# Rolled overflow path, fewer parts before and behind a branch, attention queries two batches at a time

## The chip, the cores and the metric

The kernel runs on one core of a Trainium2 chip. The core has five engines that work side by side: TensorE (PE, matrix products; its weight loads are the row PEld), VectorE (DVE), ScalarE (ACT), GpSimd (POOL) and SyncE (SP, which here only starts transfers). Transfers are carried by 16 DMA engines. The metric is device time in microseconds, lower is better; one execution was also taken by the hardware profiler.

## The reference

The reference is a transformer of two layers on x (8 batches of 100 rows, 512 wide), with a context of 8 x 361 rows, 128 wide. Each of its four parts is added to x after a layer normalisation:

- attention 1: 16 heads of 32, causal, keys and values from the first 100 rows of the context;
- a mixture of 8 experts: a gate takes the two best of 8 scores of each row, and y = sum of w_e * (silu(x W1_e) * (x W2_e)) W3_e, hidden width 352;
- attention 2: 16 heads; its queries go through Wq, w_kc_q and W_qr, its keys are the rotated context through W_kr, softmax over 361 rows, values through w_kc_kv and Wo;
- a feed-forward part with a gate, hidden width 1408, weights and rows quantised to 8-bit steps.

## The kernel before

**Tiling.** The 800 rows are seven tiles, six of 128 and one of 32 (`ROWS`). Products are in float32, so that each product is two passes on PE in the profile. Results land in eight PSUM banks (`bank`), from which ACT or DVE copies them; `evacuate` gives them to the two in turn.

**Order.** Up to the branch, and again from behind it to the end of attention 2's projections, the order on PE, DVE and ACT is that of the source (`manual_schedule`). The order on SP and POOL, and that of attention 2's loop, is made by the scheduler of the framework. Each queue runs in order.

**Attention 1.** Two products on zeros stand ahead of everything. `queries0(b, n, parts)` makes the queries of n batches, in one or two banks; batches 0 and 1 are made one by one with 100 columns, the others in pairs with 200.

**Gate and slots.** `rank_choices` finds each row's two experts on DVE, `give_slots` counts a place for each choice in the 240 slots of its expert (`CAP`), and POOL writes the rows to these slots in DRAM (`x_slot`) with indirect transfers, one for each tile and choice: ten for tiles 0 to 4, then four for tiles 5 and 6. DVE then computes `spilt`: whether an expert has more than 240 rows.

**The branch.** PE, DVE, ACT and POOL read `spilt` (`values_load`, L879) and jump (`If`, L886). The path behind the condition computes the mixture in a general way, written out for 8 experts x 7 tiles; with these inputs it isn't taken. Past the branch, SP fetches the slots of experts 0 and 1 (`fetch`, L960).

**Folding.** The weights Wq, w_kc_q and W_qr of attention 2 are multiplied into one matrix `wqf`, two heads (a pair) at a time, between other work. A pair has three parts: `fold_first` (L705, and the copy a_p), `fold_second` (L723, and the copy f_p), `fold_third` (transposes, L733). `fold_load` loads the weights of a pair, three pairs ahead at most. Pair 0 is folded ahead of the branch, pair 1's first part too; pair 1's other parts and pair 2 behind it; pairs 3 to 7 within experts 0 to 4.

**Experts.** For each expert: `gate_and_up(0)`, (1), (2) (L1053), then the transposed rows of the next expert (`columns_of`, L985), then the down product (L1117). Between them DVE quantises weights of the last part: rows of gate and up (`quantise_next`), and in experts 0 to 3 a quarter of w_down, `quantise_down(*down_in)`, which was loaded into a single buffer `dn` (L828) and is turned by a transfer (L150). `load_expert(e + 2)` comes when expert e has used its weights.

**Attention 2.** A batch has 1600 rows (16 heads x 100) in 13 tiles. For a tile: scores (L1312), maximum (L1314), exponential (L1318), division on POOL or DVE (L1321), transposes (L1327), evacuation to pT; each 400 columns of pT give a product with the context (L1333). Work behind the scores is three tiles late. The queries of the next batch are made by `queries(b + 1)` at tile 8 (in batch 0 at tile 2), with L1300: 64 rows, two heads in two halves of the array, 100 columns.

## Time and profile before

| | us |
|---|---|
| median of 3 runs | 683.59 (680.39 to 683.71) |
| the profiled execution | 684.2 |
| its span | 682.5 |
| queries of batches 0 and 1 (L269, 100 columns) | 10.25 to 17.5 |
| last PE work before the branch | 126.6 |
| PE goes on | 134.65 |
| first fetch of slots issued | 135.79 |
| expert 0 starts | 144.27 |
| expert 5 starts | 238.58 |
| attention 2's loop | about 347 to 537 |

The span is what the engines show between the first and the last instruction; the execution's time has 1.7 us more around it. A row of the profile's groups gives the line, the engine, the operation, the tile written and those read, the shapes and the count. "Idle before" is how long the engine stood still ahead of it, and what released it. The clock row gives the share of its full clock that PE was granted. A row that ends in q (PEldq, SPq) is that of an engine's sequencer, which starts instructions and runs branches.

### The profile page before, as it was taken

What the parts mean: (1) busy time and instruction counts of PE and PEld (TensorE: products, weight loads), DVE (VectorE), ACT (ScalarE), POOL (GpSimd) and SP (SyncE); (2) the same over time, 40 slices, a digit from 0 to 9 for tenths busy, and PEclk for the clock granted to TensorE, in tenths of its full rate; (3) what the DMA queues carried; (4) which work ended last, traced back from release to release, by engine and by line L of the source; (5) the groups of instructions that cost most, each with busy time, mean ns of one, the idle gap of its engine ahead of it and who ended that gap; (6) DMA issues with size and microseconds to landing.
All of it is one profiled execution on the core that took longest, in us unless ns stands there. A gap on an engine that the chain in (4) does not pass through costs nothing.

```text
span 682.5 us, 10210 instructions
## 1 busy us (share of the span) xinstructions
PE 647.0 (95%) x3637; PEld 417.3 (61%) x3637; DVE 420.7 (62%) x1059; ACT 245.2 (36%) x557; POOL 184.1 (27%) x197
## 2 busy tenths in 40 slices
PE   8999997499998999999999999999999999999995
PEld 6767755367765677568866666666666644444442
DVE  4875698326665453254168877776676356566687
ACT  3654444141221211231155555455555322221140
POOL 2222231601110022138424243324333102221021
PEclk9999999589999999999999999999999999999998
DMA  8700293699999999664200211110000120111211
GB/s 303 237 17 18 99 331 108 244 301 190 271 288 321 322 254 275 131 193 122 63 1 17 57 44 42 31 35 12 1 11 1 46 83 8 30 29 30 49 37 61
DMA packets 80312, 80.41 MB, mean 118 GB/s; under 512 B 41283, under 2 KB 54135, under 8 KB 80127
## 3 DMA queue, kind: packets, MB, share of 16 engines
q1 hardware_dynamic: 76543, 70.97, 35.8%
q0 software_dynamic: 3712, 8.72, 6.6%
q8 instruction: 30, 0.49, 0.3%
q14 instruction: 27, 0.22, 0.1%
HBM read 56.36 MB, written 16.50 MB: 107 GB/s over the span
## 4 chain that ended last, share of the span: by engine, by line
PE 65%; DVE 7%; DMA 3%; POOL 2%; issue 2%; ACT 1%; SPq 0%; POOLq 0%; ACTq 0%; DVEq 0%
PE bank L357 12%; PE bank L1053 10%; PE bank L1333 10%; PE bank L1312 7%; PE bank L1267 6%; PE bank L1117 5%; PE bank L1327 4%; PE bank L1457 3%; POOL e L1321 2%; PE bank L1300 2%; DVE nm L1314 1%; PE bank L705 1%; PE bank L723 1%; DMA dn<-in_wdn 1%; PE bank L985 1%
## 5 line engine op out<-in xcount | busy, mean ns | idle before, releaser
L1321 POOL TENSOR_SCALAR e<-e,rs 128x361 f32<-128x361 f32 (+1 forms) x56 | 67.3, 1203 | 134.9 <-DVE rs L1320 134.2
L357 PE MATMUL bank<-wvo,ctxT 128*128 128x512 f32 x192 | 83.9, 593 | 0.0
L1312 PE MATMUL bank<-kvT,qe 128*128 128x361 f32 (+1 forms) x208 | 82.0, 477 | 0.0
L1053 PE MATMUL bank<-xgT,w 128*128 128x240 f32 (+1 forms) x384 | 76.5, 371 | 1.6 <-ACT xgT L989 0.9
L1053 PEld LDWEIGHTS bank<-xgT,w 128*128 128x128 f32 (+1 forms) x384 | 63.8, 181 | 16.7 <-issue 9.0
L1333 PE MATMUL bank<-pT,kvr 121*128 121x400 f32 x192 | 70.4, 502 | 1.8 <-DVE pT L80 1.8
L1318 ACT ACTIVATE e<-bank,nm 128x361 f32<-128x361 f32 (+1 forms) x104 | 58.7, 564 | 29.8 <-DVE nm L1314 21.0
L1327 PEld LDWEIGHTS bank<-ident,e 128*121 128x121 f32 (+1 forms) x312 | 47.3, 183 | 33.7 <-POOL e L1321 7.8
L1314 DVE TENSOR_REDUCE nm<-bank 128x1 f32<-128x361 f32 (+1 forms) x104 | 54.9, 528 | 20.3 <-PE bank L1312 19.2
L357 PEld LDWEIGHTS bank<-wvo,ctxT 128*128 128x128 f32 x192 | 36.2, 190 | 43.1 <-issue 42.6
L1128 POOL DMA_INDIRECT x_acc<-y,place x16 | 24.4, 1525 | 128.5 <-ACT y L1127 125.0
L1327 PE MATMUL bank<-ident,e 128*121 128x128 f32 (+1 forms) x312 | 52.8, 279 | 2.1 <-POOL e L1321 2.1
L1474 POOL TENSOR_TENSOR hid<-g,u 128x512 f32<-128x512 f32 (+1 forms) x17 | 20.5, 1214 | 111.1 <-ACT g L1465 74.8
L1333 PEld LDWEIGHTS bank<-pT,kvr 121*128 121x128 f32 x192 | 33.9, 190 | 21.3 <-issue 1.9
L1117 PE MATMUL bank<-w,hT 128*128 128x512 f32 (+3 forms) x96 | 43.3, 596 | 2.2 <-DVE hT L1077 2.2
L1267 PE MATMUL bank<-xT,wqf 128*128 128x256 f32 (+1 forms) x192 | 43.8, 389 | 0.7 <-ACT xT L1252 0.7
L322 POOL TENSOR_TENSOR s<-s,rs 100x800 f32<-100x800 f32 x16 | 24.4, 1523 | 71.2 <-DVE rs L321 30.5
L1267 PEld LDWEIGHTS bank<-xT,wqf 128*128 128x128 f32 x192 | 36.2, 190 | 7.4 <-ACT xT L1252 0.9
L1312 PEld LDWEIGHTS bank<-kvT,qe 128*128 128x128 f32 (+1 forms) x208 | 32.5, 186 | 9.4
L82 ACT COPY pT<-bank 121x384 f32<-121x384 f32 (+1 forms) x51 | 23.7, 465 | 31.9 <-PE bank L1327 31.3
L80 DVE COPY ctxT<-bank 128x400 f32<-128x400 f32 (+2 forms) x23 | 13.2, 574 | 34.1 <-PE bank L1267 24.8
L1117 PEld LDWEIGHTS bank<-w,hT 128*128 128x128 f32 (+3 forms) x96 | 16.8, 183 | 22.9 <-issue 16.4
(251 smaller groups left out, 1020.2 us busy)
## 6 DMA issues: line engine op xcount, KB each, us to landing
w<-in_w SPq DMA_DIRECT2D x8, 1408.0 KB
gu<-in_wgu SPq DMA_DIRECT2D x22, 256.0 KB
w<-in_w SPq DMA_DIRECT2D x16, 256.0 KB
wq_p<-in_wq SPq DMA_DIRECT2D x8, 512.0 KB
wo<-in_wo SPq DMA_DIRECT2D x8, 512.0 KB
x_slot<-zeros SPq DMA_DIRECT2D x1, 3840.0 KB
kq_p<-in_wkcq SPq DMA_DIRECT2D x16, 192.0 KB
dn<-in_wdn SPq DMA_DIRECT2D x4, 704.0 KB
```

The source lines that it names most:

```text
L322: nc.gpsimd.tensor_tensor(part, part, rs.unsqueeze(2).to_broadcast([S, 8, S]), ALU.mult)
L357: nc.tensor.matmul(po[:, :D], lhs[:, c, ds(t * P, r)], rhs[:, c, :], start=(c == 0), stop=(c == chunks - 1),)
L1053: nc.tensor.matmul(po, w12_e[:, c, cols], xgT[:, c, :], start=(c == c0), stop=(c == c1 - 1))
L1117: nc.tensor.matmul(py[i][:n], hT[:mr, m, ds(s0, n)], w3_e[:mr, m, :], start=(m == 0), stop=(m == 2))
L1128: d = nc.gpsimd.indirect_dma_start(out=x_acc, out_offset=bass.IndirectOffsetOnAxis(ap=place[:, 0:1], axis=0), in_=y, in_offset=None, compu ...
L1267: nc.tensor.matmul(pq[:, i, :], wqf[:, c, ts(p0 + i, P)], xT[:, c, :], start=(c == 0), stop=(c == KC - 1),)
L1312: nc.tensor.matmul(ps[:r, :L], qe[:, ds(k0, r)], kvT, start=True, stop=True)
L1314: d = nc.vector.tensor_reduce(nm[:r], ps[:r, :L], AX.X, ALU.max, negate=True)
L1318: nc.scalar.activation(e[:r], ps[:r, :L], AF.Exp, bias=nm[:r], accum_out=sm[:r])
L1321: (nc.vector if odd else nc.gpsimd).tensor_scalar_mul(e[:r], e[:r], rs[:r])
L1327: nc.tensor.transpose(pt[:LP, c, :r], e[:r, ds(c * (LP - 1), LP)], ident[:r, :r])
L1333: nc.tensor.matmul(pc[:, :VC], kvr[:, c, :], pT[:, c, ts(j, VC)], start=(c == 0), stop=(c == LC - 1))
```

## The change

- **Attention 1**: the queries of batches 0 and 1 are made together, 200 columns each; a third product on zeros stands at the start.
- **Scatter**: for the last tile (32 rows) the second choices are copied under the first, rows and places, and one transfer of 64 rows writes both: 13 transfers, not 14.
- **Folding**: pair 1 is finished ahead of the branch; two whole pairs (2 and 3) stand behind it; four pairs (4 to 7) stay in experts 0 to 3. Those four are made by `fold_beside`: the two heads in two column halves of the array, with 128 columns moving, which gives the transposed product; `fold_turn` turns it back. Their parts stand one place later in an expert.
- **Branch**: the general path is two nested loops at run time instead of 56 written-out blocks, with gathered weights and rows; the other side of the branch is placed behind it (`preferred_fallthrough_block=True`), and SP reads `spilt` and branches too. A Silu of one column is computed by ACT between.
- **Attention 2**: `queries` makes two batches at a time (200 columns), in four parts; two parts at tiles 6 and 9 of every second batch. pT is two halves with three buffers in turn, and the tile that lies across column 800 is evacuated in two pieces.

The arithmetic for these inputs is the same apart from the order in which the folded product is formed. The order on SP comes out differently in the experts: in the built program `wq_p` of a pair and the first weights of expert e + 2 now stand ahead of the turned quarter of w_down and the next load of `dn` in experts 1 and 2, where they stood behind them.

```diff
@@ -429,7 +431,7 @@
-    for _ in range(2):
+    for _ in range(3):
...
     take_columns(1)
-    queries0(0, 1)
-    queries0(1, 1)
+    queries0(0, 2)
     first_norm(2, NT)
...
+
+        if t1 == NT:
+            r = ROWS[-1]
+            nc.vector.tensor_copy(x_all[ds(r, r), NT - 1, :], x_all[:r, NT - 1, :])
+            nc.vector.tensor_copy(to_i[0][ds(r, r), NT - 1 :], to_i[1][:r, NT - 1 :])
         for t in range(t0, t1):
-            r = ROWS[t]
-            for k in range(2):
+            r = ROWS[t] if t < NT - 1 else 2 * ROWS[t]
+            for k in range(2 if t < NT - 1 else 1):
                 d = nc.gpsimd.indirect_dma_start(
...
+    def fold_beside(i, wq_p, kq_p, qr_p):
+        pa = bank()
+        for c in range(CQ // P):
+            for j in range(2):
+                nc.tensor.matmul(
+                    pa[ds(R1 * j, R1), :P], qr_p[:, j, c, :], kq_p[:, j, c, :],
+                    start=(c == 0), stop=(c == CQ // P - 1),
+                )
+        t_p = fw.tile([P, P], F32, tag="t_p", name=f"t_p{i}", bufs=1)
+        nc.scalar.copy(t_p, pa[:, :P])
+        return i, wq_p, t_p
+
+    def fold_turn(i, wq_p, t_p):
+        pa = bank()
+        nc.tensor.transpose(pa[:, :P], t_p, ident)
+        a_p = fw.tile([P, P], F32, tag="a_p", name=f"a_p{i}", bufs=2)
+        nc.scalar.copy(a_p, pa[:, :P])
+        return i, wq_p, a_p
...
     fold_third(*part)
     gate_scores(5, 7, xT)
-    loads = loaded.pop(0)
-    pa = fold_head(*loads, 0)
+    part = fold_first(*loaded.pop(0))
     rank_choices(5, 7)
     give_slots(5, 7)
     nc.vector.tensor_reduce(most, pn[:, :NE], AX.X, ALU.max)
     spilt = gp.tile([P, 1], I32, tag="spilt", name="spilt")
     nc.vector.tensor_scalar(spilt, most, float(CAP), None, ALU.is_gt)
+    part = fold_second(*part)
+    fold_third(*part)
     close_atw()
     close_at()
...
         spilt[0:1, 0:1], min_val=0, max_val=1,
         engines=[
             mybir.EngineType.PE, mybir.EngineType.DVE, mybir.EngineType.Activation,
-            mybir.EngineType.Pool,
+            mybir.EngineType.Pool, mybir.EngineType.SP,
         ],
     )
-    with tc.If(spills > 0, preferred_fallthrough_block=False):
+    with tc.If(spills > 0, preferred_fallthrough_block=True):
+
+
         sp, close_sp = open_pool("spill", side="right")
...
+        with tc.For_i(0, NE, 1, hint_engines=()):
+            nc.gpsimd.iota(at_x, pattern=[[0, 1]], base=0, channel_multiplier=1)
+            w12_e = sp.tile([P, KC, 2 * HE], F32, tag="spw", name="spw")
+            for c in range(KC):
...
+            with tc.For_i(0, NT, 1, hint_engines=()):
+                x_t = sp.tile([P, D], F32, tag="spx", name="spx")
+                gathered(x_t, x_all_rows, at_x)
...
-    part = fold_copy(*loads, fold_head(*loads, 1, pa))
+    nc.scalar.activation(most, ln_eps, AF.Silu)
+    part = fold_first(*loaded.pop(0))
     following = fold_first(*loaded.pop(0))
     part = fold_second(*part)
     following = fold_second(*following)
...
         part = None
         gate_and_up(0)
         if loaded:
-            part = fold_first(*loaded.pop(0))
+            part = fold_beside(*loaded.pop(0))
             if pairs_left:
                 loaded.append(fold_load(pairs_left.pop(0)))
         quantise_next()
         gate_and_up(1)
         if part:
-            part = fold_second(*part)
+            part = fold_turn(*part)
         if e < KC:
             turn_down(*quantise_down(*down_in))
             if e + 1 < KC:
                 down_in = load_down(e + 1)
         gate_and_up(2)
+        if part:
+            part = fold_second(*part)
         quantise_next()
         if e + 2 < NE:
             experts[e + 2] = load_expert(e + 2)
         else:
             load_wo(*((0, 1, 2) if e + 2 == NE else (3, 4)))
-        if part:
-            fold_third(*part)
         if e == KC + 1:
             load_wo(5, 6, 7)
         if e + 1 < NE:
             turned = columns_of(e + 1, slots[e + 1])
             gates_next = choices(e + 1, slots[e + 1])
+        if part:
+            fold_third(*part)
...
-    def queries(b):
-        qe = a1w.tile([P, 2, HP * S], F32, tag="qe", name=f"qe{b}")
-        for half in range(2):
+
+    def pair_tile(b):
+        return a1w.tile([P, 2, 2, HP * S], F32, tag="qe", name=f"qe{b}")
+
+    def queries(b, qe, parts):
+        for part in parts:
             pe = [bank(), bank()]
-            for i in range(4):
+            for i in range(2):
                 for par in range(2):
                     nc.tensor.matmul(
-                        pe[par][:, ts(i, S)], wkr_sb[ds(R1 * par, R1), 4 * half + i, :],
-                        qr[ds(R1 * par, R1), 4 * half + i, ts(b, S)], start=True, stop=True,
+                        pe[par][:, ts(i, 2 * S)], wkr_sb[ds(R1 * par, R1), 2 * part + i, :],
+                        qr[ds(R1 * par, R1), 2 * part + i, ds(b * S, 2 * S)],
+                        start=True, stop=True,
                     )
-            nc.vector.tensor_copy(qe[:, 0, ts(half, VC)], pe[0][:, :VC])
-            nc.scalar.copy(qe[:, 1, ts(half, VC)], pe[1][:, :VC])
-        return qe.rearrange("p a q -> p (a q)")
+            for par, copy in ((0, nc.vector.tensor_copy), (1, nc.scalar.copy)):
+                copy(
+                    qe[:, :, par, ds(2 * part * S, 2 * S)].rearrange("p b (i q) -> p i b q", i=2),
+                    pe[par][:, : 4 * S].rearrange("p (i b q) -> p i b q", i=2, b=2),
+                )
+
+    def of_batch(qe, k):
+        return qe[:, k].rearrange("p a q -> p (a q)")
...
-        evacuate(pT[:, :, ds(k0, r)], pt[:LP, :, :r])
+        for half in range(2):
+            c0, c1 = max(k0, half * 2 * VC), min(k0 + r, (half + 1) * 2 * VC)
+            if c0 < c1:
+                evacuate(
+                    pT[half][:, :, ds(c0 - half * 2 * VC, c1 - c0)], pt[:LP, :, c0 - k0 : c1 - k0]
+                )
     def values(b, j, kvr, pT):
+        pT = pT[j // 2][:, :, ts(j % 2, VC)]
         pc = bank()
         for c in range(LC):
             nc.tensor.matmul(
-                pc[:, :VC], kvr[:, c, :], pT[:, c, ts(j, VC)], start=(c == 0), stop=(c == LC - 1)
+                pc[:, :VC], kvr[:, c, :], pT[:, c, :], start=(c == 0), stop=(c == LC - 1)
...
-    qe = queries(0)
+    pair = pair_tile(0)
+    queries(0, pair, range(HP // 2))
+    qe = of_batch(pair, 0)
     for b in range(B):
         more = b + 1 < B
-        pT = a1w.tile([LP, LC, BROWS], F32, tag="pT", name=f"pT{b}")
+        pT = [
+            a1w.tile([LP, LC, 2 * VC], F32, tag="pT", name=f"pT{b}_{half}", bufs=3)
+            for half in range(2)
+        ]
         if more:
             kvr_next = context_rows(b + 1)
         for i, (k0, r) in enumerate(BTILES):
             e = scores(qe, kvT, k0, r, i % 2)
             late.append(lambda a=(b, i, e, kvr, pT): behind(*a))
             drain(3)
-            if more and i == (8 if b else 2):
-                qe_next = queries(b + 1)
+            if more and b % 2 and i in (6, 9):
+                if i == 6:
+                    pair_next = pair_tile(b + 1)
+                queries(b + 1, pair_next, range(2) if i == 6 else range(2, HP // 2))
...
-            qe, kvr, kvT = qe_next, kvr_next, kvT_next
+            if b % 2:
+                pair = pair_next
+            qe, kvr, kvT = of_batch(pair, (b + 1) % 2), kvr_next, kvT_next
```

## The prediction

> **What bounds the kernel now.** I read the page first, then stretches of it, then single waits and the order of the built programs. The page's busy row and the clock in its 40 slices:

> ```profile
> PE 647.0 (95%) x3637; PEld 417.3 (61%) x3637; DVE 420.7 (62%) x1059; ACT 245.2 (36%) x557; POOL 184.1 (27%) x197
> PEclk9999999589999999999999999999999999999998
> ```

> TensorE carries the span, and the only hole before the tail is around slice 8: the branch. Time saved on TensorE is time of the kernel wherever TensorE waits for nobody, so I ask for each touched stretch whether it does. These rows are start:end, length, busy time of PE, PEld, DVE, ACT, POOL, the granted clock, the DMA share and GB/s:

> ```profile
> 10.14:17.30 7.16, 7.16 (x67) 7.16 (x66) 4.01 (x10) 1.09 (x2) 0.00 (x0) 1.00 1.05 351
> 126.60:134.65 8.05, 0.01 (x1) 0.00 (x1) 2.18 (x15) 0.00 (x0) 5.57 (x6) 0.50 0.56 203
> 199.05:220.31 21.26, 18.69 (x89) 12.74 (x89) 11.83 (x30) 3.72 (x8) 3.57 (x3) 1.00 1.13 300
> 220.31:238.58 18.27, 18.27 (x88) 12.98 (x89) 8.67 (x29) 3.69 (x8) 2.50 (x2) 1.00 1.09 323
> 238.58:253.79 15.21, 15.21 (x70) 11.01 (x68) 8.14 (x24) 2.38 (x6) 3.04 (x2) 1.00 1.16 262
> 347.50:537.00 189.50, 186.09 (x953) 122.58 (x951) 139.85 (x390) 104.03 (x298) 67.27 (x56) 1.00 0.09 23
> ```

> Row 1 is queries0: PEld is busy all the time, so weight loads bound it. Row 2 is the branch: PE does nothing for 8 us. Rows 3 to 5 are experts 3, 4 and 5: with a fold 18.27, without 15.21, so a fold costs 3.06; expert 3 took 3 us more. In all of them the DMA engines are full (share over 1). Row 6 is attention 2: 186 of 189.5 us on PE, DMA idle.

> Why expert 3 is long, from the chain that ended last:

> ```profile
> 204.44 7.48 DMA dn<-in_wdn
> 211.92 0.02 issue
> 211.94 1.63 DVE amax L145
> ...
> 217.65 1.98 PE bank L1117 x4
> ```

> The load of the last quarter of w_down lands at 211.92, VectorE has waited for it 3.94 us, hT of that expert stands behind it on VectorE, and the down product resumes 5.7 us after the landing. The one before it came 1.07 us late too, without harm to PE. So a queue of transfers is a second bound of the experts, just behind PE.

> **The change part by part** (minus is gain; sums against the profiled execution of 684.2, span 682.5).

> *1. Queries of attention 1.* The timeline has both shapes:

> ```profile
> 10.25 7.29 PE L269 MATMUL bank<-xnT,wq_sb 128*128 128x100 f32 x64
> 26.52 5.68 PE L269 MATMUL bank<-xnT,wq_sb 128*128 128x200 f32 x32
> ```

> 64 passes of 100 columns become 32 of 200: 7.29 - 5.68 = **-1.6**. The scores behind them wait for the copy of the second half (0.5), covered by the mask products (0.84). If VectorE, which has five norms to do after this (2.36), is what the next products wait for, it still starts earlier, because its scale follows the same copies. Bounds -0.8 to -2. The added warm-up product is two passes of about 0.65 between 4.44 and 5.72, where PE waits for xn anyway: 0.

> *2. Branch.* The sequencers' own rows:

> ```profile
> L879 PEldq TENSOR_LOAD <-spilt x1: 749/749/749, 129.2 to 129.2; - x1
> L886 PEldq COMPARE_BRANCH  x2: 89/1917/3745, 130.4 to 130.7; - x2
> L886 DVEq COMPARE_BRANCH  x2: 51/53/55, 130.1 to 130.3; - x2
> ```

> spilt is there at 129.16, PE reads it in 0.75, and its jump over the unrolled path takes 3.745; DVE's and ACT's take 0.05. [...] The rolled body on PE is 39 products instead of 56 such blocks, so I take the short jump: -3.65. [...]
> The scatter saved: POOL's are 1.26 apart, so the last ends 1.26 earlier (132.6), and the fetch of slots, issued at 135.79 after it drained, goes out at about 134.5. Price: two VectorE copies ahead of spilt, 32x516 by the row of a 128x512 SBUF operation (0.55) and 32x1 (0.144): +0.7, spilt at 129.86; the scatter starts at 131.7, so they don't delay it. SyncE now reads spilt and jumps as well; everything it issues is queued behind that. Even with PE's long jump it would be through at 134.4, before the scatter has drained: 0.
> PE then resumes at 129.86 + 0.75 + 0.25 = 130.9 instead of 134.65. Pair 1's second and third part (1.76 + 0.58 + 0.7 at half clock) fit between 126.6 and 129.8, in the wait for spilt: 0. Behind the branch there is now one first part more: 2 x 2.8 at half clock, 130.9 to 136.5. The clock was back 6.9 us after PE resumed (half from 121.05 to 141.53), so I put it at 137.8: second parts until 139.4, copy 0.6, third 0.6, end 140.6 against 142.5: **-1.9**. [...] The Silu table load goes ahead of the branch on ACT, done before a_p is asked for: 0.

> *3. Experts.* Four folds in them instead of five: **-3.06**. fold_beside: the first part was 12 passes in 1.28. With 64-column weights the nearest row is the 64-wide weight load of L1053, 8 in 0.61, so 12 in 0.91 at worst, 12 x 55 = 0.66 if both column halves run at once (a pass streams 0.85 ns a column: L357's 192 passes of 512 in 83.9); the turn adds a pass of about 0.15. **-0.35** each, -1.4 for four (bounds 0 to -2).
> A new wait: pair 4 is asked for in expert 0, not 1. Its load is the last of 3.6 MB issued from the fetch on; at the rates before (0.28 MB in 136:138, then about 0.55, 0.56, 0.78, 0.76, 0.63 per 2 us) it lands near 146.8, and PE wants it near 145.8: +1.
> Now the queue. In the built program SyncE issues w12 of expert e+2, and one wq_p, ahead of the transposed w_down and the next w_down load in experts 1 and 2; before, these went first. The down loads for experts 2 and 3 get 1.44 MB more ahead of them (the wq_p falls into a hole at 156:158, where the queue waited for PE). At 0.38 MB/us, what 212:218 moved, that is +3.8. Landing of the last: 211.92 - 1.25 + 3.8 = 214.5; with 8.4 from landing to the next expert as before (211.92 to 220.31), expert 4 starts at 222.9 and not at 220.31. Expert 2's load lands at 193.2 by the same sum, PE can bear 189.5 (10.3 after the expert's start, as expert 3 could), so that expert already loses about 3.7. So the -1.9, -1.4 and the +1 are swallowed: expert 4 starts 2.6 later, and with its fold gone (-3.06) the experts and the branch come to **-0.5** in all. Bounds: -8.4 (no stall at all: -1.9 + 1 - 3.06 - 1.4 - 3) and +9.7 (below).

> *4. Queries of attention 2.* 256 passes of 100 columns in 16.3 us, 2.03 per batch, 63 ns each:

> ```profile
> 382.34 2.03 PE L1300 MATMUL bank<-ctxT,wkr_sb 64*128 64x100 f32 x32
> ```

> The stream alone, two row halves at a time, would be 43 ns (0.85 a column); their weight loads (14.9 us for 256, 58 ns) bound it. With 200 columns the stream is 85 and covers the load: 32 x 85 = 2.7 to 32 x 105 = 3.4 (if the 20 ns over the stream stay) for two batches, not 4.06: -1.35 to -0.7, four times. L269 at 200 columns came within 8 ns of its stream (5.68 / 32), so I take -1.1 each: **-4.5**. PE is busy 98% here, so it counts. Against it: one more evacuation per batch (the tile across column 800 is cut in two, about 0.3 us on ACT or DVE), hidden by 50 us of idle DVE; three half buffers of pT for two whole ones: the half that is reused was read a batch earlier. 0, at worst +1.

> The sum: -1.6 - 0.5 - 4.5 = -6.6. The profiled execution gives 677.6; it lies 0.6 above the median, so **677.0**.

> **The rivals.**
> *Experts bound by PE.* If transfers come in time (the queue slots let them overlap better than my in-order sum), the stalls vanish: -1.6 - 8.4 - 4.5 = -14.5, 669; with expert 3's old stall kept, -11.5, 672. For it: loads earlier by 1.25. Against: share over 1 throughout.
> *Slower: w_down falls behind a full queue.* In 168:172 the queue moved 60 GB/s, so the mean may be the right price, not the best rate: w12 and wq_p, 1.97 MB at 0.14 MB/us = 14 us; landing 224.7, expert 4 at 233.1, +12.8 - 3.06 - 1.6 - 4.5 = +3.6: 687. It decides from a landing at about 221 (no gain) and 224.5 (0.5% slower).
> *Attention 2 gains nothing,* because copies of queries now bunch up on DVE (74% busy) in every second batch: -1.6 - 0.5 - 0.5 = -2.6, 681.
> *The jump stays long:* experts start about 1.8 later than before, but expert 4's start is the transfers'; 677 to 679.

> **How the numbers follow.** The measurement can tell 0.5%, 3.4 us: below 680.2 is faster, above 687 slower. Chances: my sum 0.48 (own range 674 to 680.5), experts bound by PE 0.22, attention 2 without gain 0.14, long jump 0.06, w_down far behind 0.10. Leaving out one in ten on each side gives 669.5 to 684. Faster: 0.45 + 0.22 + 0.03 + 0.04 = 0.74; slower 0.10; the rest, 0.16, within 0.5%.

> **What would show it.** L269's first block near 5.6; PE's second branch row near 0.1 and PE's products resuming near 131 less 1.6; expert 0 near 140.8; waits of VectorE for dn in experts 2 and 3 of more than 1.07 and 3.94 in all; fold_beside near 0.8; queries of a pair near 2.9. I am wrong if dn is in time, if PE's jump is still long, or if attention 2 keeps its 189.5 us.

## The result, and the profile after

| | before | after |
|---|---|---|
| median of 22 runs each | 682.42 us (680.39 to 683.71) | 675.27 us (672.26 to 682.40) |
| ratio | | 0.9896, 95% interval 0.9882 to 0.9911 |
| profiled execution, its span | 684.2, 682.5 | 681.28, 679.5 |

The change gains 1.0%, 7.15 us between the medians; the forecast was 677.0. An execution more than 1.5% above the fastest of its kernel counts as slow and is left out of the ratios (one of the 22 here, and the profiled one of the run layout below). Two things in the table ask for care. The times of before lie within 3.3 us, those of after within 10.1. And the profiled execution of after is the second slowest of its 22, so it shows what happens in a bad execution, not in the usual one. A second profile of the same program (the experiment after_again) turned out to be a quiet one, and the two together tell the story. Spans by stage, each from the first product of one stage to the first of the next (the second profile's first stage holds a delay of some 3.3 us ahead of the branch, of a kind that every profile taken together with it has; see the end):

| stage | before | after | after, second profile |
|---|---|---|---|
| to the transposes for expert 0 (start, branch, folds) | 142.37 | 141.63 | 144.65 |
| experts 0 to 4 | 90.22 | 90.22 | 81.57 |
| expert 5 to attention 2 | 112.58 | 112.63 | 112.64 |
| attention 2 | 194.49 | 191.74 | 189.99 |
| the rest | 142.84 | 143.28 | 143.25 |
| span | 682.5 | 679.5 | 672.1 |

The page of the first profile, busy row and clock:

```profile
PE 646.9 (95%) x3476; PEld 415.3 (61%) x3483; DVE 419.9 (62%) x1065; ACT 245.0 (36%) x565; POOL 183.5 (27%) x196
PEclk9999999589999999999989999999999999999998
```

TensorE is busy for 646.9 us, as before (647.0), although it has 161 products fewer. The clock tells why in part: besides the hole at the branch there is a second one, an 8 in the 21st slice, which before did not have. The stretches that answer to those shown of before (start:end, length, busy time of PE, PEld, DVE, ACT, POOL, granted clock, DMA share, GB/s): queries0, the branch, experts 3, 4 and 5, attention 2.

```profile
10.73:16.24 5.51, 5.51 (x32) 5.47 (x33) 4.05 (x10) 0.50 (x1) 0.00 (x0) 1.00 1.05 346
126.23:131.02 4.79, 3.10 (x11) 1.04 (x9) 2.77 (x17) 1.54 (x3) 3.55 (x5) 0.50 0.50 197
200.09:221.76 21.67, 18.79 (x89) 12.30 (x90) 11.82 (x30) 3.97 (x9) 3.03 (x3) 0.96 1.09 320
221.76:237.89 16.13, 16.13 (x69) 11.75 (x69) 8.68 (x29) 2.35 (x5) 2.52 (x2) 0.95 1.19 244
237.89:253.10 15.21, 15.21 (x69) 11.02 (x68) 8.14 (x24) 2.38 (x6) 3.04 (x2) 1.00 1.08 317
346.80:536.22 189.42, 185.22 (x843) 120.78 (x840) 140.14 (x395) 103.58 (x302) 67.24 (x56) 0.99 0.08 23
```

The branch stretch is now 4.8 us and mostly filled with a fold. Expert 4 lost its fold (16.13 against 18.27) and would be at 15.2 like expert 5, but its clock is 0.95. Expert 3 got longer, 21.67 against 21.26, although its fold got cheaper. The chain that ended last has the reason, the same load as before:

```profile
206.39 0.58 SPq L152
206.97 0.05 issue
207.03 6.35 DMA dn<-in_wdn
213.39 1.63 DVE amax L147
...
219.10 2.85 PE bank L1175 x4
```

The timeline of VectorE and that of TensorE show the waits themselves, one in expert 2 and one in expert 3. VectorE of before, with 5.0 us in the two, stands first; then VectorE of after, with 7.4 us; then TensorE of after:

```profile
190.68 1.62 DVE L145 TENSOR_REDUCE amax<-dn 128x1 f32<-128x1408 f32 x1 [1.07 <-DMA dn<-in_wdn]
...
211.94 1.62 DVE L145 TENSOR_REDUCE amax<-dn 128x1 f32<-128x1408 f32 x1 [3.94 <-DMA dn<-in_wdn]
```
```profile
191.72 1.62 DVE L147 TENSOR_REDUCE amax<-dn 128x1 f32<-128x1408 f32 x1 [2.68 <-DMA dn<-in_wdn]
...
213.39 1.62 DVE L147 TENSOR_REDUCE amax<-dn 128x1 f32<-128x1408 f32 x1 [4.69 <-DMA dn<-in_wdn]
```
```profile
197.42 1.98 PE L1175 MATMUL bank<-w,hT 96*128 96x512 f32 x4 [0.87 <-DVE hT L1133]
...
219.10 2.85 PE L1175 MATMUL bank<-w,hT 96*128 96x512 f32 x4 [2.88 <-DVE hT L1133]
```

The four products at 219.10 take 2.85 us and not 1.98: after TensorE's 2.88 us of waiting the clock was halved for about 3.4 us. In the second profile no row of VectorE waits for dn at all; the last of them reads

```profile
207.91 1.61 DVE L147 TENSOR_REDUCE amax<-dn 128x1 f32<-128x1408 f32 x1
```

The start, the branch and the queries of attention 2, from TensorE's timeline, its sequencer's row and the groups by line:

```profile
10.73 5.68 PE L271 MATMUL bank<-xnT,wq_sb 128*128 128x200 f32 x32 [0.68 <-ACT xnT L256]
...
131.02 5.36 PE L711 MATMUL bank<-qr_p,kq_p 128*128 128x64 f32 x24 [1.01 <-PEq L913]
...
344.89 2.98 PE L1361 MATMUL bank<-ctxT,wkr_sb 64*128 64x200 f32 x32
```
```profile
L913 PEldq COMPARE_BRANCH  x1: 353/353/353, 130.4 to 130.4; - x1
```
```profile
L1361 PE MATMUL bank<-ctxT,wkr_sb 64*128 64x200 f32 x128 | 12.7, 341 | 0.0
```

TensorE's jump is 0.353 us where it was 3.745, and the queries of attention 2 take 12.7 us in all where they took 16.3.

### The profile page after: what moved, and what is told of

Its sections match the earlier page's. It is cut to its first block, busy times and chain, and to the rows that moved or that the text cites. A ratio compares the mean times of both kernels' runs of the same rounds, so it can differ in the third digit from the quotient of the medians.

```text
span 679.5 us, 9904 instructions
## 1 busy us (share of the span) xinstructions
PE 646.9 (95%) x3476; PEld 415.3 (61%) x3483; DVE 419.9 (62%) x1065; ACT 245.0 (36%) x565; POOL 183.5 (27%) x196
## 4 chain that ended last, share of the span: by engine, by line
PE 63%; DVE 7%; DMA 7%; POOL 1%; issue 1%; ACT 1%; SPq 0%; ACTq 0%; POOLq 0%; DVEq 0%
PE bank L359 12%; PE bank L1406 9%; PE bank L1379 9%; PE bank L1109 8%; PE bank L1325 6%; PE bank L1175 5%; PE bank L1394 5%; PE bank L1539 3%; DMA dn<-in_wdn 2%; PE bank L1361 1%; DMA gu<-in_wgu 1%; DMA qr_p<-in_wqr 1%; POOL e L1388 1%; DVE amax L147 1%; PE bank L711 1%
## 5 line engine op out<-in xcount | busy, mean ns | idle before, releaser
L359 PE MATMUL bank<-wvo,ctxT 128*128 128x512 f32 x192 | 83.9, 593 | 0.0
L82 ACT COPY pT<-bank 121x384 f32<-121x384 f32 (+1 forms) x63 | 28.2, 447 | 42.4 <-PE bank L1394 42.3
L80 DVE COPY ctxT<-bank 128x400 f32<-128x400 f32 (+2 forms) x31 | 17.7, 572 | 37.0 <-PE bank L1325 26.0
```

Of the source, the lines that this page charges most:

```text
L82: nc.scalar.copy(dst, src)
L359: nc.tensor.matmul(po[:, :D], lhs[:, c, ds(t * P, r)], rhs[:, c, :], start=(c == 0), stop=(c == chunks - 1),)
```

## The experiments

My theory, from the prediction: gains at the start, the branch and attention 2, with the queue of transfers taking back what the experts would gain. The rivals: that the experts are bound by TensorE, that w_down falls further behind, that attention 2 gains nothing, that the jump stays long. The twelve runs were made in three groups of four kernels, each group with before beside it; the third group ran on another chip than the first two. In the first group before took 682.5 us. In the second and third it took 687.4 and 686.6 us, and in every profile made there a copy of ScalarE ahead of the branch came late (see the end). So ratios, and not times, are compared between groups, and the start of the profiles within one group only.

### Queries of attention 2 as before

```
-    queries(0, pair, range(HP // 2))
-    qe = of_batch(pair, 0)
+    qe = queries(0)
...
-            if more and b % 2 and i in (6, 9):
-                if i == 6:
-                    pair_next = pair_tile(b + 1)
-                queries(b + 1, pair_next, range(2) if i == 6 else range(2, HP // 2))
+            if more and i == (8 if b else 2):
+                qe_next = queries(b + 1)
```

> The changed kernel with the queries of attention 2 of before (one batch at a time, 100 columns a pass, whole pT). If the wider passes are what attention 2 gained, its stretch from the first context product to the last values is 194.5 us again instead of 191.7, the row of the queries 16.3 us instead of 12.7, the hole of 2.3 us before the first transposes is gone, and the time is 2.5 to 4 above the changed kernel's 675.3: 678 to 679. If attention 2 gained nothing and the gain lies in the branch and the experts, the time stays at 675.

Measured: 677.89 us (676.94 to 680.01), ratio 0.9932 (0.9915 to 0.9949), against 0.9896 for the change whole. Attention 2 takes 194.49 us in its profile, to the hundredth what it took before. So this part is worth about 0.36%, 2.5 us, in the medians, and the rival "attention 2 gains nothing" is out. The gain that is left, 4.6 us of the median, lies ahead of attention 2. (The profiles have more for this part: attention 2 of after is 2.75 us shorter than in before in the first profile, 4.50 in the second.) Unlooked for: this program issues the same transfers in the same order in its experts, and waited only 0.39 us for w_down.

### The first pair's queries in two halves

```
-    queries(0, pair, range(HP // 2))
+    queries(0, pair, range(2))
...
             drain(3)
+            if b == 0 and i == 2:
+                queries(0, pair, range(2, HP // 2))
```

> The changed kernel, but only two of the four parts of the first pair's queries stand ahead of the first scores; the other two stand behind the third tile's scores, as the queries of batch 1 did before. If the hole of 2.3 us at 350 to 353 and the half clock of one window behind it (about 1.7 us) come from having nothing to put between the first scores and the first transposes, both shrink: hole below 1, no half clock at 353, time 2 to 3 us below the changed kernel: 672 to 673.5. If the start of attention 2 is bound by the exponentials and their scaling anyway, the products only wait elsewhere: 675.

The rows that led to it: in the first profile of after, TensorE waits 2.27 us at the start of attention 2, since nothing is left to put between the first scores and the first transposes. The clock is full until 350:352 and then halved for one stretch of 3.4 us, as these two-microsecond windows of after say (clock is the third number from the end):

```profile
350.00:352.00 2.00, 0.49 (x2) 0.00 (x0) 1.53 (x5) 2.00 (x8) 0.69 (x1) 1.00 0.00 0
352.00:354.00 2.00, 1.24 (x5) 0.98 (x6) 0.58 (x3) 0.02 (x1) 0.71 (x1) 0.80 0.00 0
354.00:356.00 2.00, 2.00 (x6) 1.41 (x6) 1.02 (x4) 0.73 (x2) 1.19 (x1) 0.50 0.00 0
356.00:358.00 2.00, 2.00 (x11) 1.41 (x9) 1.50 (x4) 1.07 (x5) 0.76 (x1) 0.85 0.00 0
```

The timeline of the variant:

```profile
341.91 1.62 PE L1361 MATMUL bank<-ctxT,wkr_sb 64*128 64x200 f32 x16
343.61 0.85 PE L1379 MATMUL bank<-kvT,qe 128*128 128x361 f32 x2
345.16 0.59 PE L1394 MATMUL bank<-ident,e 128*121 128x128 f32 x3 [0.71 <-POOL e L1388]
```

Measured: 672.93 us (672.47 to 673.38), ratio 0.9861 (0.9845 to 0.9877). The hole is 0.71, no clock is lost, and attention 2 takes 189.82. Now the second profile of the unchanged kernel: it has the hole of 2.27 us at 344.86 to 347.13, too, but kept the full clock, and its attention 2 takes 189.99:

```profile
347.13 0.59 PE L1394 MATMUL bank<-ident,e 128*121 128x128 f32 x3 [2.27 <-POOL e L1388]
```
```profile
342.29:345.70 3.41, 2.58 (x8) 1.32 (x8) 2.92 (x8) 3.36 (x8) 0.01 (x1) 1.00 0.00 0
345.70:349.11 3.41, 1.98 (x10) 1.33 (x10) 1.66 (x6) 1.11 (x6) 2.01 (x2) 1.00 0.00 0
```

So the hole itself costs almost nothing (0.17); what costs is the half clock. The same hole brings it in the first profile and not in the second, and the traces show what decides: where the hole lies on a grid. In each profile the granted clock changes only at instants that are whole multiples of 3.41 us apart (in after at 117.68, 141.57, 220.08, 223.49, 353.20 and 356.61). The hole of the first profile, 350.49 to 352.76, lies whole between two points of this grid (349.79 and 353.20). In the second a point of it, 345.70, cuts the hole in two, 0.84 and 1.43 us, as the two rows say (0.83 of 3.41 us without work on TensorE, then 1.43). Nine profiles have this hole. In the four that lost clock (after, layout, dn_ahead, dn_ahead_2) it lies whole between two points; in the five that did not (after_again, unrolled, unrolled_dn, unrolled_dn_2, dn_fold_first) a point cuts it, with at most 1.43 us on one side. Attention 2 of dn_ahead, dn_ahead_2 and layout took 191.45, 190.97 and 193.05 (layout has another wait of 0.89 us in it); of unrolled 190.06. So the theory holds for the clock and falls for the hole. By the two profiles of after the clock is worth at most 1.75 us. The median fell by 2.3; the rest may be that none of these four executions waited long for w_down.

### The general path unrolled again

```
-    with tc.If(spills > 0, preferred_fallthrough_block=True):
...
+    with tc.If(spills > 0, preferred_fallthrough_block=False):
...
```

Under it stands the unrolled body of before in place of the loops.

> The changed kernel with the unrolled general path of before behind the branch, and the layout that went with it. If TensorE's short jump comes from the small rolled body, its branch row shows some 3.7 us again, its products resume near 134.6 instead of 131.0, and expert 0 starts about 3.5 later. If transfers set the experts' pace, about 1 to 2 of that is still there at expert 4 (now 221.8): 676 to 677.5. If TensorE does, all 3.5 is: 679.

TensorE's branch row:

```profile
L913 PEldq COMPARE_BRANCH  x2: 95/1820/3544, 130.1 to 130.4; - x2
```

Measured: 681.36 us (675.24 to 684.41), ratio 0.9973 (0.9946 to 0.9999). The long jump is back (3.544), products resume at 134.23 and the transposes for expert 0 start at 145.37, 3.7 later than in after. But the median is 6.1 above that of after, more than the jump and above both forecasts, and the times spread over 9 us. Its profile, of one of its faster executions (677.38), waits 3.88 us for w_down. Two costs were mixed here, so the jump's own had to be measured with the queue set free, below.

### w12 behind w_down

```
-        if e + 2 < NE:
+        if e in (1, 2):
+            with tc.issue_after(dn_issue[0]):
+                experts[e + 2] = load_expert(e + 2)
+        elif e + 2 < NE:
             experts[e + 2] = load_expert(e + 2)
```

Here `dn_issue[0]` is the load of w_down that was issued last.

> The changed kernel with w12 of experts 3 and 4 issued behind the loads of w_down's third and fourth quarter instead of ahead of them (1.44 MB each); otherwise the same. If the queue ahead of these loads is what VectorE's waits for dn are made of, its waits fall from 7.4 us in two to below 4, expert 4 starts near 219 to 220 instead of 221.8 and the time is 1.5 to 3 below: 672.5 to 674. If the queue is full whatever the order, w12 of expert 4 is late in its turn, expert 4 starts at 221.5 to 224, and the time is 675 to 678.

SyncE's queue at the end of expert 2, first of after, then of its second profile, then of this variant (L484 is w12 of expert 4, L152 the transposed copy of w_down's third quarter, L855 and L857 the load of its last quarter, for which VectorE waits in expert 3; the second column is how long SyncE was held by issuing it):

```profile
198.26 0.41 SPq L484 DMA_DIRECT2D w<-in_w  x1
198.77 8.21 SPq L152 DMA_TRANSPOSE w2q<-dn_q  x1
207.03 0.57 SPq L855 DMA_DIRECT2D dn<-in_wdn  x1
```
```profile
194.59 0.40 SPq L484 DMA_DIRECT2D w<-in_w  x1
195.10 4.34 SPq L152 DMA_TRANSPOSE w2q<-dn_q  x1
199.49 0.57 SPq L855 DMA_DIRECT2D dn<-in_wdn  x1
```
```profile
194.23 2.57 SPq L152 DMA_TRANSPOSE w2q<-dn_q  x1
196.84 0.58 SPq L857 DMA_DIRECT2D dn<-in_wdn  x1
...
199.45 0.38 SPq L484 DMA_DIRECT2D w<-in_w  x1
```

Measured: 674.54 us (673.12 to 675.56), ratio 0.9887 (0.9870 to 0.9905). No wait for dn is left in the profile, experts 0 to 4 take 82.57 us and not 90.22, and w12 is not late in its turn. In the prediction I had put the price on bytes in front of the load. The rows say that much of it is paid at the issue: with 1.44 MB queued right ahead, SyncE is held for 8.21 or 4.34 us by the transposed copy, 2.57 without, and the load leaves that much later. Over all profiles this copy takes 4.04 to 8.21 us in the six that have w12 ahead of it, 1.85 to 2.65 in the seven that have it behind. Of the seven (this variant and those below that are built on it) none waits more than 0.3 us for w_down; of the six three wait 3.88 us or more. The queue is what the waits are made of. But the median gains little over 0.9896, because in most executions of after the waits are small: the 7.4 us of its first profile are not typical.

### The same kernel again, and both edits together

> The changed kernel once more, unchanged, for a second profile. Its profiled execution of 681.3 us waited 7.4 us for w_down; two variants with the same order of transfers in the experts waited 0.4 and 0.8. If the waits for w_down differ from one execution to the next, this one shows 0.3 to 5 us of them, its expert 5 starts between 230 and 236 instead of 237.9, and the median is again 674 to 676. If they come with the program, they are 7.4 again and expert 5 starts at 238.

Measured: 677.31 us (673.81 to 680.86) beside a before of 687.36, ratio 0.9859 (0.9823 to 0.9894). In the profile no wait for dn; experts 0 to 4 take 81.57 us, the least of all runs. This program's waits do differ from one execution to the next. Of the six profiles with this order of transfers, three waited 0, 0.39 and 0.80 us (after_again, q2_as_before, q2_split), three 3.88, 6.69 and 7.4 (unrolled, layout, after). What decides it I could not find: the transposed copy held SyncE for 6.8 and 8.2 us in two of the late ones, but for 4.0 in the third. The lateness is older than this copy: SyncE issued w12 of expert 4 4.1 to 6.6 us after the transposes for expert 3 began in the three late ones, 1.6 to 2.5 us after them in the others.

> Both edits together: the first pair's queries split around the third tile, and w12 of experts 3 and 4 behind the loads of w_down. If they act on different stretches, they add up to the undisturbed pace of both: no wait for w_down, no hole of 2.3 us, 671 to 672.5 and little spread. If the split alone already has what is to be had, because w_down is in time in most executions, 672.5 to 673.5, the median of the split alone, with less spread.

Measured: 677.87 us (675.84 to 678.14), ratio 0.9843 (0.9812 to 0.9875), no wait for dn, attention 2 at 190.73 (no clock lost; a wait of 0.96 us in its second batch is new). The forecast was made for a before of 682.4, where the ratio gives 671.7, inside it. But in the median it is not better than the unchanged kernel beside it (677.31), and the two intervals overlap. Its spread is 2.3 us where that one's is 7.0.

### What makes the jump long, and what it costs

```
-    with tc.If(spills > 0, preferred_fallthrough_block=True):
+    with tc.If(spills > 0, preferred_fallthrough_block=False):
...
```

> The changed kernel with its small rolled path, but laid out as before: the path stands in line, and the usual case jumps over it. If the length of the path made the jump long, TensorE's branch stays at 0.35 us or below 1, products resume near 131, and the time is 675. If it was the layout, the branch row shows 3.7 again, products resume at 134.4, and the time is 678 to 682, as with the unrolled path.

TensorE's branch row:

```profile
L913 PEldq COMPARE_BRANCH  x2: 95/200/304, 134.4 to 134.7; - x2
```

Jumping over the rolled body costs 0.304 us, over the unrolled one 3.544. The length of the path makes the jump long, not the layout. The time, 681.61 us (675.93 to 686.26, ratio 0.9893, 0.9843 to 0.9944), spreads over 10 us, and its profile, of the slowest of the six executions, has 6.69 us of waiting for dn; it says nothing on the jump.

> The unrolled general path of before (TensorE's long jump) and w12 behind w_down's loads. With the unrolled path alone the time was 681.4 and its executions spread over 675 to 684. If the long jump costs TensorE's time and nothing else, this is 674.5 (the same order of transfers with the short jump) plus 3.5 to 4: 678 to 678.5, and no wait for w_down over 1 us. If the later start of the fetch and of the experts is what makes w_down late, waits for w_down are still there, and it is 680 to 682.

> The order of transfers of dn_ahead again, as the base of the other three, which stand beside it here: ratio to before 0.9887 as the first time if nothing but the order counts; no wait for w_down over 1 us in its profile.

> The same with the unrolled general path, so TensorE's long jump, beside its base. If the 3.5 us of the jump are TensorE's time from the branch to the end, this is 3.5 above the base. If the wait for pair 4's load in expert 0 (1.2 to 1.8 us in the runs with the short jump, none in the first profile of this one) takes back what the early start gave, it is 1.7 to 2.3 above.

The first stood beside split_dn in the second group: 679.75 us (679.01 to 680.15), ratio 0.9880 (0.9846 to 0.9913); its times can't be held against its two forecasts, since before ran 5 us longer there. The other two were measured side by side in the third: 677.68 (675.03 to 679.18), ratio 0.9868 (0.9846 to 0.9889), against the forecast 0.9887, and 678.81 (678.45 to 680.00), ratio 0.9888 (0.9872 to 0.9905). None of the three profiles waits for dn. In the medians the long jump costs 1.1 us, 0.2%, with intervals that overlap. TensorE's rows behind the branch, dn_ahead_2 and then unrolled_dn_2:

```profile
134.76 5.36 PE L711 MATMUL bank<-qr_p,kq_p 128*128 128x64 f32 x24 [1.35 <-PEq L915]
...
147.18 3.48 PE L1111 MATMUL bank<-xgT,w 128*128 128x240 f32 x16 [0.92 <-ACT xgT L1046]
...
151.95 0.87 PE L731 MATMUL bank<-kq_p,qr_p 128*64 128x128 f32 x10 [0.82 <-DMA qr_p<-in_wqr]
```
```profile
138.94 2.79 PE L711 MATMUL bank<-qr_p,kq_p 128*128 128x64 f32 x12 [4.97 <-issue]
...
142.32 2.79 PE L711 MATMUL bank<-qr_p,kq_p 128*128 128x64 f32 x12 [0.59 <-ACT a_p L719]
...
152.21 1.05 PE L1083 MATMUL bank<-xgT,w 128*128 128x240 f32 x4 [0.92 <-ACT xgT L1018]
```

Products resume 4.2 later and expert 0 starts 5.0 later with the long jump. The short jump then waits for pair 4's load in expert 0, the long one doesn't, and by expert 5 the difference is 3.7 (228.21 and 231.88). In these two profiles 1.4 of it goes the other way later: attention 2 took 190.97 and 190.06 (the first lost a stretch of clock at the hole, the second did not), the rest 143.27 and 142.73. So the jump's 3.7 us are seen in place as far as expert 5. That they reach the end in full is not shown; the medians show 1.1.

### The fold of before in the experts

```
-            part = fold_beside(*loaded.pop(0))
+            part = fold_first(*loaded.pop(0))
...
-        if part:
-            part = fold_turn(*part)
```

> The base with the folds of the experts as before: the first part in 12 passes of 64 columns with no product to turn it. By my sum (0.35 us for each of four) it is 1.4 above the base. By the experts' pace in the profiles (18.27 with a fold before, 17.61 after) it is 0.66 for each, 2.6 above. If transfers set the pace of experts 0 to 3, nothing.

Measured: 677.25 us, ratio 0.9869 (0.9850 to 0.9888), the same as its base (677.68, 0.9868). In the profiles an expert with a fold takes 17.83 us from transposes to transposes; 17.61 with fold_beside; 18.19 before. So fold_beside itself is worth 0.22 for each. The other 0.36 is left for the second and third part standing behind the last gate_and_up; this was not measured alone. Four times 0.22 is 0.9 us, too small to be seen in the time.

### A version with all that helped

The base of dn_ahead, the split of q2_split, and the fold of pair 4 in expert 0 behind its second gate_and_up:

```
-        if loaded:
+        if loaded and e:
+            part = beside()
...
         gate_and_up(1)
...
+        if not e:
+            part = beside()
```

Here beside() is the fold with the next load behind it, as before; in expert 0 the turn, the second and the third part move back by one place each.

> The base with the first pair's queries of attention 2 split, and with the fold of pair 4 in expert 0 moved behind that expert's second gate_and_up, 7 us later, so that its load has landed. If the wait for it (1.2 to 1.8 us) is TensorE's time, and the hole at the start of attention 2 too (0 to 2), this is 1.5 to 3.5 below the base. If the experts are then held by the next load (w12 of expert 2, or the slots), it is 0 to 1 below.

Measured: 675.23 us (674.20 to 677.13) beside a before of 686.57, ratio 0.9841 (0.9822 to 0.9860); its base, beside it, 0.9868. The wait for qr_p is gone, attention 2 takes 189.58, and the transposes for expert 5 start at 226.43 where the base had 228.21 (0.8 of that was there at expert 0 already). It is 2.4 us below its base, inside the expected 1.5 to 3.5, though the two intervals overlap a little, and it beats before by 1.6%. Against the change as it was made (0.9896, and 0.9859 in the second group) I have no run side by side.

## Why the prediction was right, and where it was not

The time was 1.7 us off, but two of the terms were wrong and cancelled: the start and the branch gave 1.8 to 2.8 us less than predicted, the experts in three of the profiles much more. That the number came so near is in part luck.

*1. Queries of attention 1: predicted -1.6, measured -1.1.* The duration was right (5.68). They start at 10.73 and not at 10.25: a pass over two batches needs the columns of both tiles, so the first waits 0.68 us for ScalarE's copy of the second one, xnT; before, the passes of batch 0 ran ahead of that copy. (In the second profile they start at 10.85, and the wait, 0.91, is for the load of wq_sb instead; the gain there is 1.0.) I had looked for what waits behind the passes, not for what they themselves wait for.

*2. Branch: predicted -1.9 on top of that; together -3.5, measured -0.74 in the first profile, -0.85 in dn_ahead and -1.4 to -1.7 in q2_split and q2_as_before, with the same branch.* Nearly every term held: jump 0.353, fetch issued at 134.54 (predicted 134.5), VectorE's two copies 0.56 (0.7), SyncE's jump of no harm. (The table load for Silu came behind ScalarE's jump, at 130.65, not ahead of it; it ended before the copy a_p, as predicted.) Products resumed at 131.02: right for -1.9 alone, late by what the start had gained. What failed is "the clock was back 6.9 us after PE resumed". It came back after 10.55 us in after, 10.2 in dn_ahead, 8.98 in q2_split, 8.8 in q2_as_before. The half clock also began earlier, at 117.7 and not at 121.05, so the gate's transposes and those of the fold ahead of the branch ran at half speed, and of the 1.1 us of the start 0.3 were left when the scores were through. TensorE's rows of before, then of after:

```profile
119.32 1.02 PE L577 MATMUL bank<-ident,x_all 128*128 128x128 f32 x8 [2.27 <-DVE x_all L559]
120.53 0.66 PE L733 MATMUL bank<-ident,f_p 128*128 128x128 f32 x4 [0.19 <-ACT f_p L727]
```
```profile
118.19 1.68 PE L578 MATMUL bank<-ident,x_all 128*128 128x128 f32 x8 [2.27 <-DVE x_all L560]
119.80 1.11 PE L759 MATMUL bank<-ident,f_p 128*128 128x128 f32 x4
```

Where the half clock begins and ends goes by the grid of 3.41 us, which lies differently from one profile to another (points of it at 141.57 in after, at 144.32 in its second profile); the 6.9 us read from one profile was one draw of a time that is 6.9 to 11.3 in the fourteen. An earlier restart at half clock buys half: four passes of L749 take 1.98 us there and 1.08 at full clock (at 126.23 and 114.84 in after). That the smaller body would shorten TensorE's jump to near 0.1 us was my estimate, which no run had shown; the runs show 0.353 and 0.304 us over the rolled body, 3.544 over the unrolled one.

*3. Experts: predicted to swallow the branch's gain, -0.5 for both; with the start -2.1 at expert 5. Measured there: -0.7 in the first profile, -7.7 in q2_split, -6.4 in q2_as_before.* The step that failed is "the down loads for experts 2 and 3 get 1.44 MB more ahead of them: +3.8" as a price for every execution. The mechanism was the right one: putting w12 behind removed the waits, and in the first profile the load lands at 213.4 (predicted 214.5) with 7.4 us of waiting. But half of the profiles with this order wait 0 to 0.8 us. There the rival "experts bound by PE" holds or nearly holds: experts 0 to 4 in 85.53, 83.98 and 81.57, where 90.22 - 3.06 for the fold less - 3.0 for the old stall - 4 x 0.58 for the cheaper folds gives 81.8. The fastest execution of after, 672.26, is this rival's upper figure (672), the profiled one has my waits, and the median lies between. So the runs look like a mixture of the two cases to which I gave separate chances; only the profiled executions show which case they are. The small terms: the wait for pair 4 was 1.2 in after (predicted 1), but it grows as expert 0 starts earlier. The load lets the products go on at 147.8 to 148.6 in after, dn_ahead, q2_split and q2_as_before, and in the last, which starts earliest (140.65), the wait is 1.8 and costs a stretch of half clock besides (149.51 to 152.93), so that it reaches expert 1 later than after. So the predicted -3.5 at expert 0, had it come, would by these rows have been lost here in part. The fold gained 0.58 for each (predicted 0.35, which left out what the moved second and third part gain).

*4. Attention 2: predicted -4.5, measured -4.50* (194.49 to 189.99) where the clock stays full, and -2.75 where the first scores' hole costs a stretch of clock. The rows give 3.6 for the queries themselves (3.2 for a pair, predicted 2.9). About 0.9 more lies in the other products of this stretch; I can't place it on one row. In the medians this part is worth 2.5. "At worst +1" for pT and the added evacuation wasn't needed. What I missed is that four parts of queries ahead of the first scores leave nothing to do behind them, a hole (2.27 us) that cost a stretch of clock in the four profiles of nine in which no point of the grid cuts it.

In sum: from the start to expert 0 the kernel gained 1.8 to 2.8 us less than the two terms promised; experts 0 to 4, for which the sum implies 1.4 us of loss, lost nothing in the bad execution and gained 4.7 to 8.7 in q2_as_before, q2_split and the second profile; attention 2 gained what was predicted or 1.75 less.

## What to carry to other kernels

Ask of a full queue not only how late a load comes but how surely: here a load that was just in time (waits of 0 to 7.4 us for it in six profiles) went with times that spread over 10.1 us, and one profile shows one draw of it; look at the spread of the times before explaining the profile. When a stretch is made shorter, look for the first wait of the shorter work on its own inputs, and for holes that it leaves on TensorE: here one of 2.27 us cost a stretch of half clock of 3.41 us besides, or did not, by where it fell. A long untaken path was paid on TensorE, which has to jump over it (3.745 us in before, 0.05 on VectorE); rolling it into loops shortened the jump in both layouts (0.353 and 0.304 us).
